# Layer 0 of a two-layer conditioned sequence block: maxima turned by a float32r product, values and weight halves copied by VectorE, several late pieces reordered

## The chip, the cores and the metric

The kernel runs on one core of a Trainium2 chip. A core has a matrix engine (TensorE, PE in the profile, with its weight loads as PEld), a vector engine (VectorE, DVE), an activation engine (ScalarE, ACT), a general engine (GpSimd, POOL), and SyncE (SP), which here only issues transfers. Each engine works off its own instructions in order, and engines wait for each other by semaphores. Operands lie in SBUF; a product goes to a PSUM bank, from which VectorE or ScalarE reads it. The metric is the device time of one execution in microseconds (us); a figure for a kernel is the median of several executions.

## The reference

The input is a batch of 32 sequences of 128 rows and 512 features, with a condition vector of 512 for each batch. Layer 0 is a normalised and modulated attention with 16 heads of 32 features, with the softmax divided once more by the root of 512; layer 1 is a single-head attention followed by a gated MLP, both modulated by the condition. All in float32.

```python
# layer 0
h   = (wg) * layernorm(x) + (wb)                # wg, wb: from the condition
q, k, v = split_heads(h @ Wqkv.T + bqkv)        # 16 heads of 32
att = softmax(q @ k.T) / sqrt(512)
h1  = (att @ v) @ Wp.T + bp + x
x   = sln(h1) + h1
# layer 1
h   = rmsnorm(x) * (1 + scale) + shift          # scale, shift: from the condition
x   = x + softmax((h @ q_w + q_b) @ (h @ k_w + k_b).T / sqrt(512)) @ (h @ v_w + v_b) @ proj_w + proj_b
h   = rmsnorm(x) * (1 + scale2) + shift2
x   = x + gelu(h @ mlp_w1 + mlp_b1) @ mlp_w2 + mlp_b2
```

## The kernel before

Products of full weight matrices run as three float32r products: each operand is split in a high half (rounded to float32r) and a low half (the rest), and high·high, low·high and high·low are added up in PSUM (`mm3`, L152). A tile of 128 partitions by 512 columns is the usual unit.

Layer 0 runs in 32 steps, `for s in range(STEPS)` (L1385 to L1486), after a prologue (L1300 to L1325). A step stands for one group of four batches (NG = 8 groups) and one chunk of four heads (KC = 4 chunks, 128 features). What one trip of the loop issues, in the text's order:

- `scores0(s)` (L633): per head row, a product of `over` (a matrix of ones in float32r) with the spread maxima `mT` into a bank `pst`, which puts the negative maximum and logarithm of the softmax under every score, and then 16 products of k and q on top.
- `energies(s + 1)`: the scores of the next step, row-wise, in four banks `pse`, and the row maxima `nm` by VectorE (L588). `totals(s + 1, r)` (L599): 16 exponentials on ScalarE that give only their row sums. `exponentials(s, ..)` (L654): ScalarE reads `pst` and gives the attention weights `e`.
- `heads_out(s - 1)` (L657): `e` times the values `v` into `pso`; ScalarE writes its high half (`o..h`, L676), VectorE the low half (`o..l`, L682).
- `logs(s + 1)` (L602 to L617): ScalarE's logarithm and exponential, some small VectorE operations, and at the end `nmx`, the maxima with their logarithms as a high and a low part, 128 rows by 4 heads by 32 columns (eight of them used, the others zero).
- `qk0(s + 2)`: the products for q and k of the step after next, read by ScalarE. Between them in steps 0 to 3 one piece of the output projection is split: `split_w` (L143), where ScalarE casts the high half `w0ph` (L145) and GpSimd takes the difference.
- `values0(s - 1 + G)` (L535): the values of one batch, in banks `psv`, which ScalarE copies to `v` (L542).
- `maxima(s + 1)` (L619 to L623): TensorE's transpose of `nmx` into `psm`; `spread_maxima` (L625): VectorE multiplies it out to `mT`.
- `End` for batch s − 4: the output projection `psp`, added to the residual `xe` by VectorE (L713). `Turned`: a coming batch is normalised (`x`, L411), cut into 16-bit halves by ScalarE, transposed by DMA on SP's queue (`tn`, L427), merged by VectorE (L432), modulated by ScalarE (L449), and split into `n..h` (L461) and `n..l` (L465) by VectorE.

Work for layer 1 and for the conditions is spread over the steps. `cond_half` (steps 3 and 4, L250 to L289) computes modulation rows with the weights `wc`, and at its end writes sums `shw` to memory and reads them back, spread over the partitions, as `shwt` (L286, L287). `l1_cq` (L790) loads `wk` in steps 7, 9, 11 and 13, and in the step after each VectorE sums it with a row (L795). In steps 29 to 31 `l1_vp` (L781) makes layer 1's value weights times its projection from chunks `w1c` into banks `psvp` (L787); `l1_load` loads further weights of layer 1.

The order is that of the text only for a part: each engine's order is set by a scheduler that lists the instructions again by their dependencies, so that an instruction may stand elsewhere in an engine's queue than its line suggests. Banks of PSUM come from small pools: `mm_tile` and `s_tile` (used for `pst`, `pso`, `psv`, `psvp`), and `e_bank` (for `pse`, `psm`, `psp`). A tile of a pool is free only when the last reader of its predecessor is done, so a late reader (`o..l` of `pso`) delays the next writer (`pst`).

Of the kernel before, what the change touches and what calls it, by code (L numbers as in the profile page):

```python
# [9 lines left out]
FP = mybir.dt.float32  # L10
# [33 lines left out]
def cond_seq_kernel(ctx: ExitStack, tc, x, condT, wcond, w0, w1, wk1, wm1, wm2, cols, rows, out):  # L44
# [42 lines left out]
    def load(t, src, by=None):  # L87
        (by or nc.sync).dma_start(out=t, in_=src)
        return t
# [13 lines left out]
    nc.gpsimd.memset(neghalf, -0.5)  # L103
    ones = const.tile([P, P], FP, name="ones")
    nc.gpsimd.memset(ones, 1.0)
    col = const.tile([P, NCOLS], FP, name="col")
# [4 lines left out]
    over = const.tile([P, P], FR, name="over")  # L111
    nc.vector.tensor_copy(over, ones)
    nmx = const.tile([P, 4, 32], FP, name="nmx")
    nc.gpsimd.memset(nmx, 0.0)

# [133 lines left out]
    def cond_half(h):  # L249
# [11 lines left out]
        def work():  # L261
            a, n = later["ca"], later["n"]
            ps = e_bank(f"psc{h}")
            for k in range(2):
                for j in range(4):
                    nc.tensor.matmul(
                        ps[32 * j : 32 * j + 32], cT[:, 2 * h + k, :], ws[j // 2][:, 2 * (j % 2) + k],
                        start=(k == 0), stop=(k == 1),
                    )
            nc.vector.tensor_tensor(a, ps, a, ALU.add)  # L270
            if h == 0:
                return
            for o in (0, 2 * B):
                nc.vector.scalar_tensor_tensor(
                    a[o : o + B], a[o : o + B], 1.0, n[o : o + B], ALU.add, ALU.mult
                )


            w, sums = l_tile("scw"), sm.tile([P, 1], FP, tag="v", name="shw")
            nc.vector.tensor_tensor(w[:B], a[:B], wu[:B], ALU.mult)  # L280
            nc.vector.scalar_tensor_tensor(
                w[B : 2 * B], a[B : 2 * B], 1.0, wu[B : 2 * B], ALU.mult, ALU.mult,
                accum_out=sums[B : 2 * B],
            )
            nc.sync.dma_start(out=scw, in_=w[:B])
            nc.sync.dma_start(out=shw, in_=sums[B : 2 * B])  # L286
            load(later["shw"], shw.rearrange("b o -> (b o)").partition_broadcast(P))  # L287

# [233 lines left out]
    def over_rows(name, acc):  # L522

        ps = e_bank(name)
        nc.tensor.matmul(ps, ones, acc, start=True, stop=True)
        return ps
# [7 lines left out]

    def values0(b, by_part=False, make=None):  # L535
        g, i = divmod(b, G)
        hT = hs[0, g][0]

        def done(ps):
            if i == 0:  # L540
                vs[g] = w_tile(f"v{g}", FP)
            nc.scalar.copy(vs[g][:, i], ps)  # L542

# [60 lines left out]
    def logs(s):  # L604
# [10 lines left out]
        t = nmx  # L615
        nc.vector.tensor_copy(t[:, :, :G].bitcast(FR), nm)
        nc.vector.tensor_tensor(t[:, :, G : 2 * G], nm, t[:, :, :G], ALU.subtract)  # L617

    def maxima(s):  # L619

        ps = e_bank(f"psm{s}")[:, :P]
        nc.tensor.transpose(ps, nmx.rearrange("p r j -> p (r j)"), ident)
        mT[s] = ps  # L623
# [32 lines left out]

    def heads_out(s):  # L657

        g, c = divmod(s, KC)
        e, v = es.pop(s), vs[g]  # L660
        if c == 0:
            os_[g] = w_pair(f"o{g}")
        pso = mm_tile(f"pso{s}")
        for i in range(G):
# [566 lines left out]
    with tc.manual_schedule(engines=ordered):  # L1231
# [80 lines left out]
        run(q)  # L1312
        totals(0, 3)
        first[0].turn()
        logs(0)
        first[0].parts()
        new.norm()
        run(k)
        new.halves()
        values = values0(2, make=mm_tile)  # L1320
        run(values[:4])
        maxima(0)
        spread_maxima(0)
        first[1].turn()
        run(values[4:])  # L1325
        first[1].parts()
# [43 lines left out]
        def vp(c):  # L1370
            l1_vp(chunk.pop(c), L1[3], c, s_tile if c < 3 else e_bank)

# [12 lines left out]
        for s in range(STEPS):  # L1385
            last = s == STEPS - 1
            end = End(s - G, True, nc.scalar) if s >= G else None
            scores0(s)
            if turned:
# [14 lines left out]
            if not last:  # L1404
                for r in range(1, 4):
                    totals(s + 1, r)
            if s:
                heads_out(s - 1)
# [27 lines left out]
            if s < KC:  # L1436
                split_w(W0["p"], raw["p"], s, nc.gpsimd)
            if s == KC + 1:
                cond_features()
            run(k)  # L1440
            if new:
                new.norm()
                new.halves()
            values = values0(s - 1 + G, make=e_bank if s < G else s_tile) if s <= B - G else []
            run(values[:9] if s < G else values)
            if s == STEPS - 3:
                vp(0)
            if s == STEPS - 2:
                vp(1)
                vp_load(3)  # L1450
                vp(2)
            if s == STEPS - 1:
# [10 lines left out]
            if past:  # L1463
                past.third()
            if "cq" in L1:
                L1.pop("cq")()
            staged = extras[s + 1]() if s + 1 in extras else None
            if end:
                run(end.stream())
                end.add()  # L1470
            if s == STEPS - 4:
                vp_load(0)
# [9 lines left out]
            if s == 2:  # L1482
                later["mods"] = r_tile("mods")
            if s == STEPS - 2:
                l1_load()
        heads_out(STEPS - 1)  # L1486
# [195 lines left out]
```

## Time and profile before

| | |
|---|---|
| median of 3 runs | 1421.9 us (1421.56 to 1423.0) |
| profiled execution, own time | 1421.69 us |
| its span in the profile | 1419.9 us, 25300 instructions |
| TensorE busy | 1402.5 us (99%), 8968 products |
| VectorE busy | 997.2 us (70%), 1970 instructions |
| ScalarE busy | 886.8 us (62%), 2386 instructions |
| GpSimd busy | 384.9 us (27%), 361 instructions |
| granted clock of TensorE | 0.999 |
| ScalarE's totals (L599) | 512 of 417 ns, and 512 reads of their sums of 257 ns |
| VectorE's row maxima (L588) | 128 of 684 ns |
| first `pst` of steps 0, 1, 2, 3, 4, 5, 6 | 50.05, 63.18, 77.22, 92.67, 107.59, 126.03, 142.77 us |
| first `pst` of steps 30 and 31 | 494.66, 510.82 us |

Busy time sums the durations of an engine's instructions. Those overlap at their ends: an instruction of 0.68 us can be followed by the next one 0.60 us after its start, so that what an instruction costs an engine is read from the distance of starts. "Idle before" is the time for which an engine stood still ahead of an instruction, with the instruction that let it go. The 1.8 us between the span and the profiled execution's own time lie before the first instruction and after the last.

### The profile page before, as it was taken

What the parts mean: (1) busy time and instruction counts of PE and PEld (TensorE: products, weight loads), DVE (VectorE), ACT (ScalarE), POOL (GpSimd) and SP (SyncE); (2) the same over time, 40 slices, a digit from 0 to 9 for tenths busy, and PEclk for the clock granted to TensorE, in tenths of its full rate; (3) what the DMA queues carried; (4) which work ended last, traced back from release to release, by engine and by line L of the source; (5) the groups of instructions that cost most, each with busy time, mean ns of one, the idle gap of its engine ahead of it and who ended that gap; (6) DMA issues with size and microseconds to landing.
All of it is one profiled execution on the core that took longest, in us unless ns stands there. A gap on an engine that the chain in (4) does not pass through costs nothing.

```text
span 1419.9 us, 25300 instructions
## 1 busy us (share of the span) xinstructions
PE 1402.5 (99%) x8968; PEld 1135.1 (80%) x8968; DVE 997.2 (70%) x1970; ACT 886.8 (62%) x2386; POOL 384.9 (27%) x361
## 2 busy tenths in 40 slices
PE   9999999999999999999999999999999999999998
PEld 5766888888888768888888888888888888888887
DVE  6666888888888887999887766665576556753342
ACT  4898899999998856677874454444453445423331
POOL 0113443535444234665541213000030003110000
PEclk9999999999999999999999999999999999999999
DMA  8359778777666557788879878576693767735350
GB/s 310 74 143 238 196 217 225 223 200 187 183 154 183 150 203 187 193 240 222 207 191 361 256 222 260 192 227 195 213 326 121 234 203 227 270 133 184 142 185 30
DMA packets 227879, 287.85 MB, mean 203 GB/s; under 512 B 107396, under 2 KB 138244, under 8 KB 226216
## 3 DMA queue, kind: packets, MB, share of 16 engines
q1 hardware_dynamic: 209888, 211.68, 51.5%
q10 hardware_dynamic: 17864, 74.55, 15.8%
q8 instruction: 70, 1.15, 0.4%
q14 instruction: 57, 0.47, 0.1%
HBM read 193.18 MB, written 73.60 MB: 188 GB/s over the span
## 4 chain that ended last, share of the span: by engine, by line
PE 87%; DMA 4%; ACT 4%; DVE 3%; issue 1%; POOL 1%; SPq 0%; ACTq 0%; POOLq 0%; DVEq 0%
PE acc L1087 24%; PE psh L165 21%; PE psp L165 6%; PE psq L165 5%; PE psk L165 5%; PE psV L165 5%; PE psv L165 5%; PE psT L165 5%; PE pso L667 2%; PE pss L848 2%; PE pse L575 2%; PE pst L644 2%; PE pso L165 1%; ACT unused L599 1%; DMA wc<-in_wcond 1%
## 5 line engine op out<-in xcount | busy, mean ns | idle before, releaser
L599 ACT ACTIVATE unused<-pse,nm 128x128 f32<-128x128 f32 x512 | 180.9, 417 | 10.3 <-DVE nm L588 7.9
L338 POOL TENSOR_TENSOR rn<-vn,neghalf 128x1 f32<-128x1 f32 x96 | 62.9, 655 | 453.3 <-DVE vn L336 346.4
L1025 ACT ACTIVATE c<-c,col 128x512 f32<-128x512 f32 x64 | 46.4, 725 | 142.3 <-DVE c L1050 89.0
L599 ACT ACTIVATION_READ_ACCUMULATOR unused<-pse,nm 128x1 f32 x512 | 131.8, 257 | 0.0
L423 ACT COPY tn<-x 128x1024 uint16<-128x1024 uint16 x90 | 94.1, 1047 | 59.2 <-DVE x L409 51.9
L432 DVE COPY tn<-tn 128x1024 uint16<-128x1024 uint16 x90 | 101.6, 1129 | 6.2 <-DMA tn<-tn 6.1
L1103 POOL TENSOR_TENSOR xe<-xe,row 128x512 f32<-128x512 f32 x32 | 45.4, 1449 | 202.8 <-DMA xe<-xs 182.9
L654 ACT ACTIVATE e<-pst 128x512 f32<-128x512 f32 x128 | 69.7, 605 | 30.1 <-PE pst L644 30.1
L588 DVE TENSOR_REDUCE nm<-pse 128x4 f32<-128x512 f32 x128 | 79.5, 684 | 11.8 <-PE pse L575 11.8
L963 POOL TENSOR_TENSOR wml<-wm,wmh 128x512 fp32r<-128x512 f32 x28 | 35.9, 1287 | 182.4 <-ACT wmh L956 154.9
L1040 DVE TENSOR_TENSOR c<-psh,ca 128x512 f32<-128x512 f32 x32 | 22.1, 692 | 86.7 <-PE psh L165 83.2
L326 DVE BATCH_NORM_STATS2 stn<-x 128x6 f32<-128x512 f32 x96 | 65.6, 683 | 2.7 <-DMA x<-in_x 2.7
L409 DVE TENSOR_SCALAR x<-x,rn 128x512 f32<-128x512 f32 x64 | 57.7, 902 | 7.4 <-POOL rn L338 6.7
L449 ACT ACTIVATE tn<-tn,mods 128x128 f32<-128x128 f32 x128 | 52.6, 483 | 11.7 <-DVE tn L432 11.7
L1053 DVE TENSOR_TENSOR ca<-psh,ca 128x512 f32<-128x512 f32 x32 | 22.1, 691 | 41.8 <-PE psh L165 41.8
L338 POOL TENSOR_TENSOR re<-ve,neghalf 128x1 f32<-128x1 f32 x32 | 31.4, 980 | 64.7 <-DVE ve L331 60.8
L1025 ACT ACTIVATE cb<-cb,col 128x512 f32<-128x512 f32 x32 | 23.2, 724 | 41.0 <-DVE cb L1054 41.0
L698 POOL TENSOR_TENSOR xe<-xe,row 128x512 f32<-128x512 f32 x32 | 44.9, 1403 | 1.7 <-DMA xe<-in_x 1.5
L1037 ACT COPY ca<-psh 128x512 f32<-128x512 f32 x32 | 18.4, 574 | 40.5 <-PE psh L165 40.0
L449 ACT ACTIVATE tn<-tn,mod 128x128 f32<-128x128 f32 x104 | 43.0, 491 | 0.0
L1107 DVE TENSOR_TENSOR xe<-acc,xe 128x512 f32<-128x512 f32 x32 | 21.1, 688 | 30.5 <-PE acc L1087 30.2
L1046 DVE TENSOR_TENSOR cb<-psh,ca 128x512 f32<-128x512 f32 x32 | 22.1, 690 | 24.8 <-PE psh L165 24.5
(1386 smaller groups left out, 4582.4 us busy)
## 6 DMA issues: line engine op xcount, KB each, us to landing
mod<-mod SPq DMA_DIRECT2D x32, 512.0 KB, 4.5
ur<-ud SPq DMA_DIRECT2D x64, 256.0 KB, 4.5
xs<-xe SPq DMA_DIRECT2D x60, 256.0 KB, 2.6
xe<-xs SPq DMA_DIRECT2D x60, 256.0 KB, 3.0
x<-xs SPq DMA_DIRECT2D x59, 256.0 KB, 3.5
scw<-scw SPq DMA_DIRECT2D x32, 256.0 KB, 3.9
hTd<-tn SPq DMA_DIRECT2D x32, 256.0 KB, 6.7
hT<-hTd SPq DMA_DIRECT2D x32, 256.0 KB, 5.1
```

Source lines behind the costliest of these rows:

```text
L165: nc.tensor.matmul(st["ps"], *calls[j], start=(j == 0), stop=(j == n - 1))
L326: nc.vector.bn_stats(st, t)
L338: nc.gpsimd.tensor_tensor(r, v, neghalf, ALU.pow)
L409: nc.vector.tensor_scalar(X, X, r, None, ALU.mult)
L423: nc.scalar.copy(halves.rearrange("p (e d) -> p e d", e=2), X.bitcast(U16).rearrange("p (d e) -> p e d", e=2),)
L432: nc.vector.tensor_copy(self.a.bitcast(U16).rearrange("p (f e) -> p e f", e=2), self.t.bitcast(U16).rearrange("p (e f) -> p e f", e=2),)
L449: nc.scalar.activation(dst[:, c], self.a[:, ts(c, P)], AF.Identity, bias=m[:, q + B : q + B + 1], scale=m[:, q : q + 1],)
L588: nc.vector.tensor_reduce(nm[:, r], chunks(banks[r]), AX.X, ALU.max, negate=True)
L599: nc.scalar.activation(unused[s][:, ts(i, P)], banks[r][:, ts(i, P)], AF.Exp, bias=nm[:, r, i : i + 1], scale=1.0, accum_out=total[:, r, i ...
L654: nc.scalar.activation(e, es[s][r], AF.Exp)
L1025: nc.scalar.activation(t[nm], t[nm], AF.Gelu, bias=col[:, C_B1 + f : C_B1 + f + 1], scale=1.0)
L1087: nc.tensor.matmul(accs[i], u[pa][:, ts(i, P)], wb[f // 4][pb][:, f % 4, :], start=(first and j == 0), stop=(last and j == len(PARTS) - 1),)
```

## The change

- `maxima`: the transpose of `nmx` against the identity becomes a product of `nmx` with `identr`, the identity cast to float32r. `nmx` is a float32r tile. The matrix `ones` is gone: `over` is cast from a tile of ones that VectorE fills, and stands for `ones` where columns are summed.
- Copies: the values of batch 2 in the prologue and those made in steps 0 to 3, and the four pieces `w0ph` of steps 0 to 3, are copied by VectorE instead of ScalarE.
- Prologue: the norm of the new batch stands ahead of the turn of the first one, the parts of the first batches are put off, and the maxima of step 0 are turned behind 8 of 12 value products instead of 4.
- Read-back: the load of `shwt` is taken out of `cond_half` and written three steps further on.
- Sums of `wk` (`cq`) behind the products and the residual addition of `End`.
- Last steps: in step 31 `heads_out(30)` stands ahead of `scores0(31)`, with a bank of `e_bank`; `vp(1)` takes a bank of `mm_tile`; `l1_load` is written between the loads and products of step 30.

```diff
@@ -101,17 +101,17 @@
     nc.scalar.preload_act_table_set("natural_log_exp_and_others")
     neghalf = const.tile([P, 1], FP, name="neghalf")
     nc.gpsimd.memset(neghalf, -0.5)
-    ones = const.tile([P, P], FP, name="ones")
-    nc.gpsimd.memset(ones, 1.0)
+    identr = const.tile([P, P], FR, name="identr")
+    nc.vector.tensor_copy(identr, ident)
     col = const.tile([P, NCOLS], FP, name="col")
     cT = const.tile([P, KC, B], FP, name="cT")
 
 
     pick = const.tile([P, G], FP, name="pick")
     over = const.tile([P, P], FR, name="over")
-    nc.vector.tensor_copy(over, ones)
-    nmx = const.tile([P, 4, 32], FP, name="nmx")
-    nc.gpsimd.memset(nmx, 0.0)
+    nc.vector.tensor_copy(over, warm[:, :P])
+    nmx = const.tile([P, 4, 32], FR, name="nmx")
+    nc.gpsimd.memset(nmx.bitcast(FP), 0.0)
 
 
     def split_sb(pair, sl, src, eng=None):
@@ -284,7 +284,6 @@
             )
             nc.sync.dma_start(out=scw, in_=w[:B])
             nc.sync.dma_start(out=shw, in_=sums[B : 2 * B])
-            load(later["shw"], shw.rearrange("b o -> (b o)").partition_broadcast(P))
 
         return work
 
@@ -522,7 +521,7 @@
     def over_rows(name, acc):
 
         ps = e_bank(name)
-        nc.tensor.matmul(ps, ones, acc, start=True, stop=True)
+        nc.tensor.matmul(ps, over.bitcast(FP), acc, start=True, stop=True)
         return ps
 
     def l0_row(got):
@@ -532,14 +531,14 @@
             row0, over_rows("psrow0", acc), ISD, bp, ALU.mult, ALU.add
         )
 
-    def values0(b, by_part=False, make=None):
+    def values0(b, by_part=False, make=None, copy=None):
         g, i = divmod(b, G)
         hT = hs[0, g][0]
 
         def done(ps):
             if i == 0:
                 vs[g] = w_tile(f"v{g}", FP)
-            nc.scalar.copy(vs[g][:, i], ps)
+            (copy or nc.scalar.copy)(vs[g][:, i], ps)
 
         return mm3(
             lambda: (make or s_tile)(f"psv{b}"),
@@ -613,13 +612,13 @@
         nc.vector.scalar_tensor_tensor(inv, total, ROOTD, inv, ALU.mult, ALU.mult)
         nc.vector.scalar_tensor_tensor(nm, inv, 1.0, nm, ALU.subtract, ALU.add, reverse0=True)
         t = nmx
-        nc.vector.tensor_copy(t[:, :, :G].bitcast(FR), nm)
-        nc.vector.tensor_tensor(t[:, :, G : 2 * G], nm, t[:, :, :G], ALU.subtract)
+        nc.vector.tensor_copy(t[:, :, :G], nm)
+        nc.vector.tensor_tensor(t[:, :, G : 2 * G], nm, t[:, :, :G].bitcast(FP), ALU.subtract)
 
     def maxima(s):
 
         ps = e_bank(f"psm{s}")[:, :P]
-        nc.tensor.transpose(ps, nmx.rearrange("p r j -> p (r j)"), ident)
+        nc.tensor.matmul(ps, nmx.rearrange("p r j -> p (r j)"), identr, start=True, stop=True)
         mT[s] = ps
 
     def spread_maxima(s):
@@ -654,13 +653,13 @@
             nc.scalar.activation(e, es[s][r], AF.Exp)
             es[s][r] = e
 
-    def heads_out(s):
+    def heads_out(s, make=mm_tile):
 
         g, c = divmod(s, KC)
         e, v = es.pop(s), vs[g]
         if c == 0:
             os_[g] = w_pair(f"o{g}")
-        pso = mm_tile(f"pso{s}")
+        pso = make(f"pso{s}")
         for i in range(G):
             for r in range(4):
                 rr = slice(32 * r, 32 * r + 32)
@@ -1311,18 +1310,18 @@
         q, k = qk0(1)
         run(q)
         totals(0, 3)
+        new.norm()
         first[0].turn()
         logs(0)
-        first[0].parts()
-        new.norm()
         run(k)
+        first[1].turn()
         new.halves()
-        values = values0(2, make=mm_tile)
-        run(values[:4])
+        values = values0(2, make=mm_tile, copy=nc.vector.tensor_copy)
+        run(values[:8])
         maxima(0)
         spread_maxima(0)
-        first[1].turn()
-        run(values[4:])
+        run(values[8:])
+        first[0].parts()
         first[1].parts()
         W0["p"] = w_pair("w0p")
 
@@ -1368,7 +1367,7 @@
             chunk[c] = l1_chunk(2, c)
 
         def vp(c):
-            l1_vp(chunk.pop(c), L1[3], c, s_tile if c < 3 else e_bank)
+            l1_vp(chunk.pop(c), L1[3], c, (s_tile, mm_tile, s_tile, e_bank)[c])
 
         FIRST1 = STEPS - G - 2
 
@@ -1385,6 +1384,8 @@
         for s in range(STEPS):
             last = s == STEPS - 1
             end = End(s - G, True, nc.scalar) if s >= G else None
+            if last:
+                heads_out(s - 1, e_bank)
             scores0(s)
             if turned:
                 turned.high(nc.vector.tensor_copy)
@@ -1404,7 +1405,7 @@
             if not last:
                 for r in range(1, 4):
                     totals(s + 1, r)
-            if s:
+            if s and not last:
                 heads_out(s - 1)
             if s == STEPS - 2:
                 vp_load(2)
@@ -1434,20 +1435,27 @@
             if staged:
                 staged()
             if s < KC:
-                split_w(W0["p"], raw["p"], s, nc.gpsimd)
+                split_w(W0["p"], raw["p"], s, nc.gpsimd, nc.vector.tensor_copy)
             if s == KC + 1:
                 cond_features()
+            if s == KC + 3:
+                load(later["shw"], shw.rearrange("b o -> (b o)").partition_broadcast(P))
             run(k)
             if new:
                 new.norm()
                 new.halves()
-            values = values0(s - 1 + G, make=e_bank if s < G else s_tile) if s <= B - G else []
+            values = []
+            if s < G:
+                values = values0(s - 1 + G, make=e_bank, copy=nc.vector.tensor_copy)
+            elif s <= B - G:
+                values = values0(s - 1 + G)
             run(values[:9] if s < G else values)
             if s == STEPS - 3:
                 vp(0)
             if s == STEPS - 2:
                 vp(1)
                 vp_load(3)
+                l1_load()
                 vp(2)
             if s == STEPS - 1:
                 vp(3)
@@ -1462,12 +1470,12 @@
                 ready.rest()
             if past:
                 past.third()
-            if "cq" in L1:
-                L1.pop("cq")()
             staged = extras[s + 1]() if s + 1 in extras else None
             if end:
                 run(end.stream())
                 end.add()
+            if "cq" in L1:
+                L1.pop("cq")()
             if s == STEPS - 4:
                 vp_load(0)
             coming_new = None if last else coming(s + 1)
@@ -1481,8 +1489,6 @@
                 L1["cq"] = l1_cq(CQ.index(s))
             if s == 2:
                 later["mods"] = r_tile("mods")
-            if s == STEPS - 2:
-                l1_load()
         heads_out(STEPS - 1)
         heads_high(STEPS - 1)
         heads_low(STEPS - 1)
```

## The prediction

> **What bounds the kernel now.** I read the chain of waits first, then busy time by stretch, then the timelines of the engines where the change lands. A difference of 0.2% (2.8 us of 1421.9) is about what a measurement of this kernel can tell from no change; "same" below means within it.
>
> The chain of waits by engine, and two stretches (columns: stretch, its length, then busy us and instructions of TensorE (PE), its weight loads, VectorE (DVE), ScalarE (ACT), GpSimd; granted clock; DMA share; GB/s):
>
> ```profile
> PE 87%; DMA 4%; ACT 4%; DVE 3%; issue 1%; POOL 1%; SPq 0%; ACTq 0%; POOLq 0%; DVEq 0%
> ...
> 55.00:100.00 45.00, 40.97 (x425) 31.02 (x428) 31.18 (x68) 41.47 (x154) 6.74 (x7) 1.00 0.47 98
> ...
> 260.00:340.00 80.00, 80.00 (x864) 65.16 (x864) 68.41 (x145) 73.52 (x267) 36.27 (x33) 1.00 0.73 198
> ```
>
> TensorE ends most of the span, and from step 6 of layer 0 on it has no hole (80.00 of 80.00): steps there last 14.53 to 14.57 us from one pst to the next. So a cost on TensorE counts in full in some 28 steps, work on other engines counts in steps 0 to 5 (TensorE 40.97 of 45.00), at step 9 and in the last two. After step 31 TensorE runs on without a gap, so what a step gains or loses stays to the end.
>
> In the early steps ACT has the larger share (41.47), but a share doesn't tell who waits. VectorE's timeline across the end of step 1 does (start, duration, line, and in brackets idle time before):
>
> ```profile
> 75.72 0.17 DVE L617 TENSOR_TENSOR nmx<-nm,nmx 128x16 f32<-128x16 f32 x1
> 75.81 0.54 DVE L411 TENSOR_SCALAR x<-x,mvn,rn 128x512 f32<-128x512 f32 x1
> 76.38 0.69 DVE L628 TENSOR_TENSOR mT<-psm,pick 128x512 fp32r<-128x512 f32 x1
> 76.99 0.68 DVE L682 TENSOR_TENSOR o0l<-pso,o0h 128x512 fp32r<-128x512 f32 x1
> 77.59 1.17 DVE L520 TENSOR_SCALAR wrow<-w0rp,col 128x512 f32<-128x512 f32 x1
> ...
> 82.09 2.48 DVE L588 TENSOR_REDUCE nm<-pse 128x4 f32<-128x512 f32 x4
> ...
> 92.44 0.68 DVE L682 TENSOR_TENSOR o0l<-pso,o0h 128x512 fp32r<-128x512 f32 x1
> 95.17 0.43 DVE L461 CAST n_8h<-tn 128x512 fp32r<-128x512 f32 x1 [2.05 <-ACT tn L449]
> ```
>
> From 75.72 to 84.5 VectorE never stops, and the row maxima (nm) that close this run are what ACT's totals wait for (82.87, 1.24 idle before them, released by DVE). Only at 95.17 does VectorE wait, for ACT.
>
> **The product in place of the transpose.** Each step turns the maxima once (psm, 32 times). Its neighbours in a steady step, then the nearest product by shape:
>
> ```profile
> 271.34 0.39 PE L165 MATMUL psv<-w0vh,n_16l 128*128 128x512 f32 x1
> 271.57 0.33 PE L622 MATMUL psm<-ident,nmx 128*128 128x128 f32 x1
> 271.66 0.48 PE L165 MATMUL psp<-w0ph,o2h 128*128 128x512 f32 x1
> 271.97 0.40 PE L165 MATMUL psp<-w0pl,o2h 128*128 128x512 f32 x1
> ...
> L848 PE MATMUL pss<-n_0f,T x32: 270/275/275, 554.2 to 557.7; 128*128 128x128 f32 x32
> ```
>
> The psv products are float32r and follow each other by 0.228 us for 512 columns. From psv at 271.34 to the second psp at 271.97 are 0.63, of which two wide products are 0.455: the transpose, with the slower start behind it, is worth 0.175 here, and 0.116 in steps whose psm loads its weights early (the same sum with psp 0.026 behind psm). No float32r product of 128 columns is in the trace. If time goes by columns, it takes a quarter of 0.228, 0.057, in place of 0.108 (the spacing of the other transposes, pstn): −0.05 a step. At the other end stands the fp32 product of the same 128x128 shape (pss), whose 32 take 3.6 us with two records each, 0.224 a piece: +0.116, or +0.16 if its weight load (0.19 in pss against 0.138 in psm) shows as well. Over 28 steps: −1.4 to +4.5. I take the row of the same shape, pss, with a little of the weight load: +0.125 a step, **+3.5**. This is the least certain term.
>
> [...] No run shows yet what a float32r product does here.
>
> **Prologue.** The turn of maxima 0 now stands behind 8 value products instead of 4, and the values of batch 2 are copied by VectorE:
>
> ```profile
> 47.51 0.33 PE L622 MATMUL psm<-ident,nmx 128*128 128x128 f32 x1 [0.81 <-DVE nmx L617]
> ...
> 50.83 0.78 PE L640 MATMUL pst<-mT,over 32*128 32x512 f32 x3 [0.29 <-ACT v L542]
> ```
>
> The 0.81 goes, because four more products (0.91) cover it. The copy on VectorE, idle there, ends near 49.85, ahead of the new pst. Step 0 starts its totals 0.93 earlier: **−0.93**.
>
> **Copies moved from ACT to VectorE, steps 0 to 3.** Each step moves a weight copy w0ph (ACT 0.61, start to start 0.51) and a value copy v (ACT 0.59, 0.47). On VectorE the first is a cast from SBUF like n_4h (0.42, start to start 0.43), the second reads PSUM like mT and o0l (0.68, 0.60). In the built order w0ph stands behind nmx, v between mT and o_l or the weighted sums: VectorE does 1.03 more per step ahead of the next nm.
> Step 0: VectorE is continuously busy from 61 to 69.6, so the 0.93 of the prologue is eaten: nm comes at its old time (+0.0 to +0.1).
> Step 1: 0.43 + 0.60 with 0.1 of slack ahead of an unbroken run: nm, totals and logs +0.93.
> Step 2: inherits 0.93. o0l, which frees the bank of the next pst, now lies behind w0ph and v, so pst goes from 93.27 to 95.2 (+1.95). n_8h had waited 2.05 there for ACT, and ACT has become faster, which absorbs most of the rest: nm +1.13, not +1.95.
> Step 3: v waits for the last psv, o0l queues behind v, and pst behind o0l: +2.5. Here there is no cover.
> SP's queue: a transpose by DMA (for batch 10) now stands between the halves of a conditioning weight that landed at 115.63 after 7.5 us and for which psc1 stalled 1.3. Issued 110.9 to 112.5 it lands at 116 to 120 against the stream's own +2.5; stall 0 to 2.4. In step 5 the next transposed batch (landing 137.68, then the merge, nmx and a psm stalled 1.53) shifts with the stream. I carry **+2.5** out of step 5, with 1.6 and 4.0 as ends.
>
> **The put-off read-back.** The load of shwt moves by three steps in the text, but in the built order it keeps its place on SP, straight ahead of the transpose at 128.07: **0**. If it did leave SP's queue there, that transpose could go earlier and the stall of 1.53 with it.
>
> **The layer-1 column sums (wk) behind the residual add.** At step 9:
>
> ```profile
> 187.14 0.69 DVE L795 SCALAR_TENSOR_TENSOR wk<-wk,row 128x512 f32<-128x512 f32 x1
> ...
> 187.75 0.69 DVE L713 TENSOR_TENSOR xe<-psp,xe 128x512 f32<-128x512 f32 x1
> ```
>
> xe comes 0.61 earlier, its psum bank is free sooner, and the stall of 0.48 of the energies behind it goes; that step lasts 15.45 against 14.55. **−0.6** (0 to −0.9; nothing reads wk soon).
>
> **Last steps.**
>
> ```profile
> 500.15 3.70 PE L787 MATMUL psvp<-w1r,w1c 128*128 128x512 f32 x8 [1.60 <-ACT e L654]
> 504.34 3.67 PE L787 MATMUL psvp<-w1r,w1c 128*128 128x512 f32 x8 [0.49 <-DMA w1c<-in_w]
> ...
> 513.06 1.08 PE L667 MATMUL pso<-e,v 128*32 128x128 f32 x32 [0.49 <-ACT e L654]
> ```
>
> The first psvp gets another bank and may start at 498.5, but the second still waits for a chunk landing at 504.20, issued at 495.30 behind two loads of 1 MB, and in the built order the l1_load that the text moves up stays where it was: 0 to −0.3, I take 0. The last pso now precedes the last pst, so its 0.49 and most of the ordering loss go: psvp at 514.07 becomes 513.05, **−1.05** (0 to −1.1).
>
> The other edits (one cast of the identity, a memset less, the ones matrix taken from over) lie in the first microseconds, under the loads: 0; uncovered, 0.4.
>
> **Sum.** The profiled run took 1421.69 for a span of 1419.9, 0.2 below the median 1421.9, which I neglect. The moved copies' +2.5 holds the prologue's −0.93 already. 1421.69 + 2.5 + 0 − 0.6 − 1.05 = 1422.5 without the product; with it, **1425.9**.
>
> **The rivals.**
> 1. The product is cheap, by columns: 1422.5 − 1.4 = 1421.1, or 1422.5 if it costs what the transpose did: same. For it: the wide float32r products run at 0.228 where fp32 takes two records of 0.43. Against: nothing as narrow is shown.
> 2. Faster: ACT ends the early steps, not VectorE. Each of four steps then returns 0.98 of ACT's time (0.47 + 0.51): −3.9, with −0.6 and −1.05: 1416.1 with a free product, 1419.6 with the dear one. For it: ACT busy 41.47 of 45.00, and VectorE waits 2.05 for ACT at 95.17. Against: the unbroken run to 84.5, with ACT idle 1.24 behind it. It decides where VectorE's added 1.03 falls into its idle time rather than ahead of nm and o0l, in at least three of the four steps.
> 3. The conditioning weight arrives late and adds up to 1.5 to the forecast: 1427.4.
>
> **How the numbers follow.** Forecast 0.45, its own range 1424.2 to 1427; rival 3 0.08; rival 1 0.25; rival 2 0.22. Faster by over 0.2% is below 1419.1: most of rival 2 (0.15) and rival 1 with the copies at their low end (0.04), 0.19. Same, up to 1424.7: the rest of rival 1 (0.21) and some of rival 2 with a dear product (0.07), 0.28. Slower: the forecast and rival 3, 0.53. The range, 1418.2 to 1428.2, leaves out most of rival 2's cheap half and the worst of the weight's delay.
>
> **What would show it.** Steady steps of 14.65 instead of 14.55 between psts (product dear) or 14.50 (cheap). VectorE's order nmx, w0ph, x, mT, v, o0l, and pst of steps 3 and 4 some 2 us late; if these psts come early, rival 2. Step 9 near 14.6. The wait at the psvp pair moved from e to the chunk. pso ahead of pst at the end. Wrong altogether I would be if TensorE's steady spacing were not what carries those 400 us.

## The result, and the profile after

The changed kernel takes 1425.8 us (median of 14 runs, 1423.6 to 1429.55), the kernel before 1423.22 us in the same session (1420.94 to 1424.69): ratio 1.0021, 95% interval [1.0013, 1.0029]. It is slower, by 2.6 us between the medians. The profiled run has a span of 1423.9 us against 1419.9.

Where the 4.0 us between the two spans lie, read from the first `pst` of each step and the first product of layer 1 (`psT`):

| stretch | before | after | difference |
|---|---|---|---|
| up to step 0 | 50.05 | 50.17 | +0.12 |
| steps 0 to 2 | 42.62 | 43.38 | +0.76 |
| step 3 | 14.92 | 16.88 | +1.96 |
| step 4 | 18.44 | 22.60 | +4.16 |
| step 5 | 16.74 | 15.13 | −1.61 |
| steps 6 to 29 | 351.89 | 351.81 | −0.08 |
| step 30 to layer 1 | 26.78 | 25.68 | −1.10 |
| the rest | | | −0.2 |

The time was lost in steps 3 and 4. The 24 steps from 6 on, which the forecast charged with a dear product, cost nothing on balance: step 9 gives back 0.75, and the others together lose 0.68. The chain of waits and the two stretches of the changed kernel (columns as before: length, busy us and instructions by engine, granted clock, DMA share, GB/s):

```profile
PE 94%; DVE 2%; ACT 2%; DMA 1%; issue 0%; ACTq 0%; SPq 0%; DVEq 0%
...
55.00:100.00 45.00, 39.53 (x411) 30.38 (x410) 30.79 (x69) 36.20 (x135) 7.17 (x6) 0.96 0.39 97
260.00:340.00 80.00, 80.00 (x835) 64.86 (x834) 67.60 (x146) 73.19 (x256) 32.95 (x30) 1.00 0.75 205
```

ScalarE is indeed relieved (36.20 of 45 for 41.47), and TensorE does less in the same stretch, not more. The new figure stands ahead of the DMA share: a granted clock of 0.96. Cut finer, first the changed kernel and then the one before:

```profile
90.00:95.00 5.00, 2.75 (x15) 1.54 (x17) 4.06 (x11) 4.32 (x11) 1.50 (x1) 1.00 0.23 57
95.00:98.00 3.00, 3.00 (x61) 3.00 (x60) 1.12 (x2) 1.52 (x4) 0.00 (x0) 0.51 0.49 95
118.00:122.00 4.00, 1.93 (x16) 0.40 (x16) 1.53 (x1) 3.97 (x23) 1.32 (x2) 1.00 1.06 337
122.00:125.00 3.00, 3.00 (x10) 1.39 (x6) 2.31 (x8) 1.28 (x4) 0.00 (x0) 0.56 0.06 16
```

```profile
90.00:95.00 5.00, 4.10 (x66) 2.89 (x69) 2.96 (x8) 5.00 (x11) 1.38 (x1) 1.00 0.84 142
95.00:98.00 3.00, 2.88 (x56) 2.27 (x52) 2.79 (x5) 2.09 (x9) 0.00 (x0) 1.00 0.53 53
```

Twice TensorE has holes (2.75 busy of 5, 1.93 of 4), and each time the clock that it is granted falls to one half right behind them. Summed over single microseconds, the clock missing is 1.71 us from 95 to 99 and 1.70 us from 122 to 126: 3.41 us at one half each time. Before, no such stretch lies inside the kernel; only the last 1.7 us of the span, behind TensorE's last product, run at half.

The holes themselves, on TensorE (start, duration, idle time before; `psc` is the bank of `cond_half`'s products):

```profile
91.56 0.30 PE L621 MATMUL psm<-identr,nmx 128*128 128x128 f32 x1 [0.59 <-DVE nmx L616]
...
93.55 0.47 PE L639 MATMUL pst<-mT,over 32*128 32x512 f32 x1 [0.94 <-DVE mT L627]
94.74 0.54 PE L639 MATMUL pst<-mT,over 32*128 32x512 f32 x3 [0.73 <-DVE o0l L681]
...
121.08 2.38 PE L266 MATMUL psc<-wc,cT 128*32 128x512 f32 x10 [2.08 <-DMA wc<-in_wcond]
123.39 0.80 PE L165 MATMUL psk<-n_4h,w0kh 128*128 128x512 f32 x1
123.99 0.63 PE L165 MATMUL psk<-n_4l,w0kh 128*128 128x512 f32 x1
```

In the kernel before, the same places:

```profile
92.67 1.10 PE L640 MATMUL pst<-mT,over 32*128 32x512 f32 x4 [0.65 <-DVE mT L628]
...
115.67 1.90 PE L266 MATMUL psc<-wc,cT 128*32 128x512 f32 x10 [0.24 <-DMA wc<-in_wcond]
```

The first pair waits for VectorE, in the order that the forecast read from the built program (here at the end of step 1; steps 2 and 3 have the same, with one more operation between `nmx` and `w0ph`):

```profile
76.15 0.18 DVE L616 TENSOR_TENSOR nmx<-nm,nmx 128x16 fp32r<-128x16 f32 x1
76.24 0.42 DVE L145 CAST w0ph<-w0rp 128x512 fp32r<-128x512 f32 x1
76.58 0.54 DVE L410 TENSOR_SCALAR x<-x,mvn,rn 128x512 f32<-128x512 f32 x1
77.03 0.68 DVE L627 TENSOR_TENSOR mT<-psm,pick 128x512 fp32r<-128x512 f32 x1
77.63 0.68 DVE L541 COPY v<-psv 128x512 f32<-128x512 f32 x1
78.23 0.68 DVE L681 TENSOR_TENSOR o0l<-pso,o0h 128x512 fp32r<-128x512 f32 x1
```

`w0ph` stands ahead of mT and v ahead of `o0l`, and `pst` waits for both. The last hole waits for the second half of the last piece of `wc`, which is called wc11 below, and SP's queue shows why it came late:

```profile
110.36 0.33 SPq L88 DMA_DIRECT2D wc<-in_wcond  x1
111.21 2.44 SPq L426 DMA_TRANSPOSE tn<-tn  x1
113.71 0.59 SPq L88 DMA_DIRECT2D wc<-in_wcond  x1
```

Before, both halves were issued by 108.5, ahead of the transpose:

```profile
107.37 1.12 SPq L88 DMA_DIRECT2D wc<-in_wcond  x2
108.61 2.85 SPq L427 DMA_TRANSPOSE tn<-tn  x1
```

Now the first is issued at 110.36, because its buffer is that of the raw projection weight, which GpSimd reads last, and GpSimd starts behind the copy that VectorE makes:

```profile
108.81 1.53 POOL L146 TENSOR_TENSOR w0pl<-w0rp,w0ph 128x512 fp32r<-128x512 f32 x1 [5.95 <-DVE w0ph L145]
```

In the kernel before:

```profile
105.83 1.51 POOL L146 TENSOR_TENSOR w0pl<-w0rp,w0ph 128x512 fp32r<-128x512 f32 x1 [5.07 <-ACT w0ph L145]
```

The second half is issued 5.6 us later than before and lands at 121.04, for 115.63 before. Not all of this is the copy's doing, as the whole stream is later here: step 4 begins at 110.43 instead of 107.59. The run u_w0ph3 below tells the two apart.

The end of layer 0 and step 9 went as forecast. The residual addition is ahead of the column sum, and the last pso ahead of the last pst:

```profile
192.00 0.69 DVE L712 TENSOR_TENSOR xe<-psp,xe 128x512 f32<-128x512 f32 x1 [0.25 <-issue]
192.61 0.68 DVE L794 SCALAR_TENSOR_TENSOR wk<-wk,row 128x512 f32<-128x512 f32 x1
```

```profile
509.50 3.67 PE L786 MATMUL psvp<-w1r,w1c 128*128 128x512 f32 x8 [2.00 <-ACT unused L598]
...
515.94 1.08 PE L666 MATMUL pso<-e,v 128*32 128x128 f32 x32
516.95 0.51 PE L639 MATMUL pst<-mT,over 32*128 32x512 f32 x4
```

The bracket at 509.50 names ScalarE, but the chunk `w1c` landed at 509.36: the two waits of 1.60 and 0.49 have become one of 2.00.

### The profile page after: what moved, and what is told of

Its sections match the earlier page's. It is cut to its first block, busy times and chain, and to the rows that moved or that the text cites. A ratio compares the mean times of both kernels' runs of the same rounds, so it can differ in the third digit from the quotient of the medians.

```text
span 1423.9 us, 25301 instructions
## 1 busy us (share of the span) xinstructions
PE 1406.1 (99%) x8968; PEld 1138.5 (80%) x8968; DVE 1000.3 (70%) x1980; ACT 883.4 (62%) x2377; POOL 384.4 (27%) x360
## 4 chain that ended last, share of the span: by engine, by line
PE 94%; DVE 2%; ACT 2%; DMA 1%; issue 0%; ACTq 0%; SPq 0%; DVEq 0%
PE acc L1086 24%; PE psh L165 21%; PE psV L165 6%; PE psT L165 6%; PE psp L165 6%; PE psq L165 6%; PE psk L165 5%; PE psv L165 5%; PE pss L847 2%; PE pso L666 2%; PE pst L643 2%; PE pse L574 2%; PE pso L165 2%; ACT unused L598 2%; PE psm L763 1%; PE pst L639 1%
## 5 line engine op out<-in xcount | busy, mean ns | idle before, releaser
L1102 POOL TENSOR_TENSOR xe<-xe,row 128x512 f32<-128x512 f32 x32 | 45.3, 1447 | 202.1 <-DVE u_7s L1078 117.1
L697 POOL TENSOR_TENSOR xe<-xe,row 128x512 f32<-128x512 f32 x32 | 45.0, 1408 | 0.6 <-DMA xe<-in_x 0.6
L899 POOL TENSOR_TENSOR xe<-xe,row 128x512 f32<-128x512 f32 x28 | 39.1, 1404 | 1.3 <-ACT V L126 1.3
```

## The experiments

Each ratio is to the kernel before, measured beside it; step lengths are from the profile of that kernel.

### The transpose in place of the product (u_turn)

```diff
-        nc.tensor.matmul(ps, nmx.rearrange("p r j -> p (r j)"), identr, start=True, stop=True)
+        nc.tensor.transpose(ps, nmx.rearrange("p r j -> p (r j)"), ident)
```

> The changed kernel with the maxima turned by the transpose again, all else kept. Theory (a float32r product of 128 columns costs TensorE what the transpose did, 0.122 against 0.117 where the weights come early, and its longer weight load, 0.186 against 0.138, shows as 0.04 to 0.05 in the other steps): some 27 steps give back about 1.1 us, ratio to before about 1.0013. Rival (the forecast's term: a product of this kind takes 0.125 more a step): 3.5 us come back, ratio 0.9997 or below, and steady steps go from 14.57 to 14.45.

1424.06 us, ratio 1.0013 [1.0004, 1.0022]. Steps 16 to 24 last 14.543 on the mean, against 14.557 in the changed kernel and 14.541 before; other kernels here that keep the product have 14.564 to 14.573. So the product costs 0.016 to 0.03 a step, not 0.125, some 0.4 to 0.8 us in all. The ratio fits the theory; its interval overlaps that of the changed kernel, and it is the steps' lengths that decide: the five profiles with the transpose lie between 14.539 and 14.543, the eight with one product between 14.557 and 14.573.

This run also prices the clock. Its wc11 is as late as in the changed kernel (stall 2.23), but the clock stays full behind the stall, and step 4 lasts 21.13 instead of 22.60.

### The product twice (p_twice)

```diff
         nc.tensor.matmul(ps, nmx.rearrange("p r j -> p (r j)"), identr, start=True, stop=True)
+        nc.tensor.matmul(ps, nmx.rearrange("p r j -> p (r j)"), identr, start=True, stop=True)
```

> The changed kernel with the product of the maxima issued twice in each step, the second over the first. Each steady step then shows what one more float32r product of 128 columns costs TensorE. Theory (time by columns with the weight load half hidden): 0.06 to 0.12 a step. Rival (the forecast: four times as slow for so few columns): 0.22 to 0.30 a step.

One execution alone, 1427.97 us, without a ratio. Steps 16 to 24 last 14.681: one product more costs 0.11 to 0.12. TensorE's rows of one step:

```profile
276.33 0.33 PE L621 MATMUL psm<-identr,nmx 128*128 128x128 f32 x1
276.50 0.27 PE L622 MATMUL psm<-identr,nmx 128*128 128x128 f32 x1
276.61 0.45 PE L165 MATMUL psp<-w0ph,o2h 128*128 128x512 f32 x1
```

The second product starts 0.17 after the first and psp 0.11 behind it. That is what a transpose costs, half of what the forecast took. It lies between the two ends, at twice a quarter of a wide product. Whether the columns or its own weight load (0.186) make it so, this run doesn't tell.

### The copies back on ScalarE, each alone (u_w0ph, u_w0ph3, u_v)

```diff
-                split_w(W0["p"], raw["p"], s, nc.gpsimd, nc.vector.tensor_copy)
+                split_w(W0["p"], raw["p"], s, nc.gpsimd)
```

> The changed kernel with the four weight copies w0ph on ScalarE again. SP's queue then holds both halves of wc11 ahead of the transpose of batch 10, as before. Theory (the w0ph copy of step 3, behind nmx and ca on VectorE, releases the buffer of wc11 3 us late and lets the transpose in between, so that the second half lands at 121.04 and psc stalls 2.08): the stall falls below 0.6, step 4 lasts at most 19.5 instead of 22.60, step 5 gives back some of it (back to about 16.5), and the whole is 1.5 to 3 us faster than the changed kernel: ratio to before 1.000 to 1.001. Rival (the w0ph copies cost only by VectorE's time in steps 1 to 3): step 4 keeps its stall of 2 us and steps 1 to 3 lose 0.4 each.

1422.92 us, ratio 1.0008 [0.9999, 1.0017]. Step 4 falls from 22.60 to 18.59 and psc runs through, since SP now has both halves ahead of the transpose. But step 5 takes 19.60, where 16.5 was expected: the transposed batch 11 then lands late for its merge, psm waits 1.90, and the clock falls to half from 141 to 145. The theory of step 4 holds; what step 5 gives back was underrated.

With the copy of step 3 alone back on ScalarE:

```diff
-                split_w(W0["p"], raw["p"], s, nc.gpsimd, nc.vector.tensor_copy)
+                split_w(W0["p"], raw["p"], s, nc.gpsimd, nc.vector.tensor_copy if s < KC - 1 else None)
```

> The changed kernel with only the last of the four weight copies, that of step 3, on ScalarE again. Same queue order on SP as with all four. Theory (it is the copy of step 3 alone, by the queue and the late release): step 4 at most 19.5, whole as with all four back within 0.5 us. Rival (VectorE's time in each of the steps): a quarter of what all four bring, and the stall of psc stays.

1424.14 us, ratio 1.0014 [1.0005, 1.0023]. Step 4 lasts 18.70: this one copy, by the order on SP, makes the stall of psc. The release of the buffer has little part in it: counted from the first `pst` (49.09 here, 50.17 in the changed kernel), the first half is issued 0.4 us sooner than there, the second, at 109.24, 3.4 us sooner. So most of the 3 us by which GpSimd starts later than in the kernel before is the lateness of the stream. Step 5 gives back most of the gain (18.11, with waits of 1.35 at pso and 1.44 at psm). Steps 1 to 3 stay at 14.53, 15.70 and 16.79, with the clock at half from 93 to 97. That the whole comes within 0.5 us of the one with all four back was not met in the medians (1.2), though their intervals overlap.

```diff
-                values = values0(s - 1 + G, make=e_bank, copy=nc.vector.tensor_copy)
+                values = values0(s - 1 + G, make=e_bank)
```

> The changed kernel with the value copies of steps 0 to 3 on ScalarE again (that of the prologue stays on VectorE). Theory (v stands ahead of o_l on VectorE and pst waits for o_l): the waits of pst for o_l in steps 2 to 4 (0.73, 0.73, 0.88) fall to about 0.15, step 2 to 4 starts come some 0.6 earlier each at most 1.5 in all, but the stall of psc for wc11 stays and takes most of it back: ratio to before 1.001 to 1.002. Rival (ScalarE's time decides): step 2 to 4 get longer by 0.4 each, ratio 1.003.

1423.18 us, ratio 1.0007 [0.9998, 1.0016]. Steps 2 and 3 fall to 15.10 and 14.75, and there is no half clock in step 3: taking v off VectorE shortens the holes (pst waits 0.13 for `o0l` instead of 0.73). Whether other runs keep the clock there too isn't shown: the mean clock over the 11 runs is 0.9976, hardly above the changed kernel's 0.9972. The gain was larger than expected (step 5 begins 3.5 us sooner, 1.3 of it from the start), and the ratio lies just below the range given. Step 4 lasts 23.25, as its late weight has a longer stall of 3.39, and the clock is at half from 119 to 122 behind it.

### The read-back put off in fact (s_before, s_after, s_w)

In the built order the changed line did not move the load. Here it is held by a dependency:

```diff
             if s == KC + 3:
+                nc.gpsimd.tensor_copy(later["shw"][:, :1], end.X[:, :1])
                 load(later["shw"], shw.rearrange("b o -> (b o)").partition_broadcast(P))
```

> The kernel before with the read-back of shwt held back for good: GpSimd first copies one column of step 7's residual tile into shwt, so that the load can't be issued sooner (that column is then overwritten by the load). Nothing else changes. Theory (the read-back, which waits for the sums to land in memory, holds up the transposed batch 11 behind it on SP, and that batch's merge stands on VectorE ahead of the logarithms): the transpose is issued 3 to 4 us sooner, the stall of 1.53 at psm of step 5 goes, step 5 lasts about 15.2 instead of 16.74, ratio 0.9989. Rival (the transfer of batch 11 is slow anyway, since other loads share the engines): step 5 keeps 16.5, ratio 1.000.

1427.49 us, ratio 1.0018 [1.0007, 1.0030]: slower, and the theory fell. The transpose is issued 2.3 us sooner, as wanted, and its merge waits longer than ever (SP, ScalarE's queue, VectorE, TensorE of this run):

```profile
125.73 3.52 SPq L426 DMA_TRANSPOSE tn<-tn  x1
...
125.94 0.61 ACTq L1478 DMA_DIRECT2D w2d<-in_wm  x1
...
142.54 1.82 DVE L431 COPY tn<-tn 128x1024 uint16<-128x1024 uint16 x1 [5.35 <-DMA tn<-tn]
...
145.27 0.45 PE L621 MATMUL psm<-ident,nmx 128*128 128x128 f32 x1 [4.88 <-DVE nmx L616]
```

Issued 0.2 us from a 1 MB copy in memory (`w2d`), the transpose takes 16.8 us to land, against 9.6 in the kernel before, where it follows the copy by 4. Step 5 lasts 21.56. Five of the twelve runs lie between 1421.6 and 1425.1 and seven between 1427.4 and 1429.1, and the profile is of the second group, so this shows what can happen and not what always does. Step 4, too, lasts longer here (20.01): psc waits 1.82, because the second half of wc11 lands 9.0 us after its issue instead of 7.5, with SP's queue up to there in the order of the kernel before. So a late landing can come without a change of order.

> The changed kernel with the read-back of shwt held back in the same way. Theory (in the changed kernel the late weight wc11 has taken the place of that stall: step 5 lasts 15.13 there already): the 2 us stall of psc in step 4 stays, step 5 gains at most 0.5, ratio 1.0017 to 1.0021. Rival (the put-off read-back was worth its 1.5 us in either kernel): ratio about 1.001.

1426.05 us, ratio 1.0017 [1.0008, 1.0026], as the theory had it: step 4 at 22.83, step 5 at 15.13. Here the transpose is issued 1.5 us ahead of w2d and lands in 8.2.

> The changed kernel with the read-back held back and the four w0ph copies on ScalarE. Theory (two stalls that cover one another: the late wc11 and the late batch 11; with both gone TensorE runs through): step 4 at most 18.8 and step 5 at most 15.8 (19.60 with the copies alone), some 3.5 us off the kernel with the copies alone, ratio 0.998 to 0.9990. Rival (step 5's loss there has another cause, as o_l or e): step 5 stays over 18, ratio 1.000 to 1.001.

The read-back held and `w0ph` on ScalarE: 1424.65 us, ratio 1.0022 [1.0007, 1.0036], missed. Step 4 lasts 19.90 and step 5 16.81, and the runs scatter from 1422.53, which is the profiled one, to 1432.03. The transpose again runs beside w2d (13.7 us to landing), psc waits 0.96 with both halves ahead of the transpose of batch 10, and the clock is at half from 78 to 81.

### The transfers put right (c_wc, c_before, c_dve, c_best)

One transfer for each pair of halves of wc:

```diff
-        for j in range(4):
-            load(ws[j // 2][:, 2 * (j % 2) : 2 * (j % 2) + 2], wcond[:, 2 + j, 2 * h : 2 * h + 2])
+        for j in range(2):
+            load(ws[j].rearrange("p (j k) d -> p j k d", j=2), wcond[:, 2 + 2 * j : 4 + 2 * j, 2 * h : 2 * h + 2])
```

> The changed kernel with each pair of halves of the conditioning weights loaded by one transfer of 1 MB, so that the transpose of batch 10 can't come between the halves of wc11; the copies stay on VectorE. Theory (of the 5.6 us by which the second half is issued later, 3 come from the late release of its buffer and 2.6 from the transpose in between): the load is issued near 110.4 and lands near 118 to 119, the stall of psc in step 4 falls from 2.08 to under 1, step 4 to 21 at most, step 5 goes up from 15.13 to some 16, and the whole gains 0.5 to 1.5: ratio 1.001 to 1.0017. Rival (the stall comes from the DMA engines' load, not from the order): landing still at 121, step 4 over 22, ratio 1.002.

1424.21 us, ratio 1.0020 [1.0010, 1.0030]. The stall of psc is gone (step 4 18.61, more than expected), so it was the transfer in between. The whole gained nothing: step 5 takes 18.19 with waits of 1.34 at pso and 1.56 at psm, and the clock stays at half from 92.8 to 99.6.

Read-back held, and w2d a step later, in the kernel before:

```diff
-            q2, late = divmod(s - W_FIRST, 3)
+            q2, late = divmod(s - W_FIRST - 1, 3)
```

> The kernel before with the read-back held back and the 1 MB copies w2d, issued by ScalarE in steps 4, 7, 10 and 13, one step later each. Theory (with the read-back held back alone, the transpose of batch 11 was issued 0.2 us from w2d and shared the DMA engines with it, 16.8 us to landing; without w2d beside it, it lands some 8 us after its issue): step 5 falls from 21.56 to about 15.2, psm waits for nothing, whole 3 to 6 us faster than with the read-back alone and 1.5 faster than the kernel before, ratio 0.9985 to 0.9993. Rival (the transpose is late by the mod and x loads ahead of it): step 5 stays over 18, ratio 1.001 or more.

1419.8 us, ratio 0.9987 [0.9979, 0.9996]: step 5 lasts 15.15, and psm waits for nothing. The neighbour of the transpose made the difference, not its place behind the read-back alone. It landed after 11.0 us, not the 8 expected, which was soon enough.

> The changed kernel with all three transfers put right (read-back held back, w2d a step later, wc in one load) and the copies still on VectorE. Theory (the copies on VectorE cost about 2.7 us in steps 1 to 3 by themselves, 1.5 more in step 4's pst and the late weight): steps 1 to 3 as in the changed kernel (14.5, 15.7, 16.9), step 4 at 20 to 21, step 5 15.2, ratio 0.9995 to 1.001. Rival (all of the loss is the transfers'): steps 1 to 3 shrink too, ratio 0.998 or less.

The changed kernel with all three transfers mended: 1423.21 us, ratio 1.0007 [0.9998, 1.0016]. Steps 4 and 5 are down to 18.38 and 15.60, steps 1 to 3 keep 14.53, 15.69 and 16.85, with the clock at half from 93 to 97. So the copies on VectorE cost 2.7 us in these steps by themselves (60.24 for steps 0 to 3, against 57.54 before), holes and clock together.

> The changed kernel with the transpose for the maxima, both copies on ScalarE again in steps 0 to 3, the read-back held back, w2d a step later and wc in one load; the prologue, the column sums behind the addition and the last steps stay as changed. Theory: prologue 1.1 sooner, steps 1 to 3 as before (14.0, 15.4, 14.9), step 4 at 18.0 to 18.5, step 5 at 15.2, step 9 at 14.7, the last steps 1.1 shorter: 4 to 5 us below the kernel before, ratio 0.9965 to 0.9975. Rival (other transfers take the place of w2d in step 5): step 5 or 6 over 16, ratio 0.998 to 0.9995.

The mended transfers, the transpose for the maxima, both copies on ScalarE, and the rest of the change: 1417.89 us (1416.92 to 1419.7), ratio 0.9972 [0.9962, 0.9983], the fastest here and faster than both kernels. Its profile at the places shown above:

```profile
90.00:94.00 4.00, 3.22 (x71) 2.46 (x69) 1.94 (x5) 4.00 (x9) 1.37 (x1) 1.00 0.77 106
94.00:97.00 3.00, 2.87 (x45) 2.24 (x41) 2.97 (x6) 2.09 (x11) 0.00 (x0) 1.00 0.21 45
118.00:126.00 8.00, 8.00 (x88) 6.57 (x90) 6.51 (x14) 4.50 (x9) 0.00 (x0) 1.00 0.65 49
126.00:140.00 14.00, 13.68 (x109) 10.72 (x109) 10.56 (x25) 13.44 (x49) 7.12 (x6) 1.00 0.99 235
```

The clock is full throughout. Steps 0 to 3 take 57.35, steps 4 and 5 33.45 (35.18 before).

## Why the prediction came out as it did

The forecast of 1425.9 met the median, and the sign was right, but the number is luck, twice over. Two of its terms were wrong and cancelled: step 6 begins 5.4 us late where +2.5 had been forecast, and from there to step 30 the kernel gains 0.08 where the product less the column sums should have cost about 2.9. And the forecast was a rise of 4.2 over the 1421.69 of one profiled run; beside the changed kernel the kernel before came to 1423.22, so the measured rise is 2.6. (The terms as written add up to 1426.0.)

- **The product**: forecast +3.5 (0.125 a step), found 0.016 to 0.03 a step, 0.4 to 0.8 in all. The step that failed is the choice of the row of the same shape, 0.224: a float32r product so narrow costs 0.11 to 0.12 (p_twice), like the transpose that it replaced (0.108 to 0.116). The rival that had it so (1422.5) was right on this point.
- **The copies on VectorE**: the mechanism was right. The order, the place in front of `o0l`, the waits of pst for it (0.73 in steps 2 and 3 and 0.88 in step 4, each 0.13 before) came as written. ScalarE's relief did end waits (pso had waited 0.81 and 0.87 for e in steps 1 and 2, now 0.22 and nothing), but the new ones were longer. From the first pst on, 3.4 us had been forecast to the end of step 5 (2.5 and the prologue's 0.93), and 5.3 came. What the sum lacked is the clock: 1.71 us of it missing in step 3 and 1.70 in step 4, which stand on no row of the kernel before, where TensorE is busy for 4.10 of the 5 us from 90 on (2.75 here). In time this is somewhat less. Of the 1.96 that step 3 lost, 0.77 are longer waits, which leaves 1.2; a second stretch of the same length in c_wc made that step 1.16 longer. Step 4 with the late weight but a full clock is 1.5 shorter (u_turn, p_twice). Taking the clock (2.7), the late weight (1.84) and the stall that went in step 5 (−1.53) from the 5.3, an estimate of 2.3 is left for the waits alone, less than the 3.4 forecast. A step paid 0.94 for the copies (0.34 and 0.60 from start to start), for 1.03 forecast.
- **The weight wc11** came late, as the third rival had it: stall 2.08, 1.84 more than before, inside the 0 to 2.4 given. (Before, psc stood still for 0.24; the prediction's 1.3 is the distance of two starts, 114.37 to 115.67.) Its second half was issued at 113.71 and landed at 121.04, both later than the 110.9 to 112.5 and 116 to 120 given. Step 4 is accounted for by this, the clock's 1.5 to 1.7 and the longer wait for `o0l` (0.75): 4.1 to 4.3 for a measured 4.16. In step 5 the old stall of 1.53 at psm disappeared, because the stream had become later (7.0 us at the start of step 5) than the transposed batch (issued 4.0 us later); the forecast had kept it.
- **The prologue**: 0.93 forecast. In nine of eleven profiles with this prologue pst starts at 48.8 to 49.1, against 50.05 to 50.63 in the three with the old one, 0.9 to 1.8 sooner. In the profile of the changed kernel (50.17) and of s_after (50.24) the gain doesn't show, because their first weight products ran late (first eight 6.04 us in the changed kernel, 3.87 before). An estimate is that the clock made them late: in the changed kernel these products start 0.85 us apart up to 9.40 and 0.43 apart from 10.00 on, and the trace's record of the clock begins, at full, at 9.73; in the kernel before they start 0.43 apart from 5.38 on, and the record begins at 5.05. In s_after each microsecond from 6 to 9 holds parts of three products, in u_turn each one from 6 to 8 parts of four.
- **The read-back**: 0 forecast and 0 found, as it kept its place. The remark that moving it would free the stall of 1.53 was wrong as it stood: alone it made the kernel slower, and only with w2d out of the way did it gain.
- **The column sums**: −0.6 forecast, −0.75 found in step 9. Against this, steps 11, 13 and 15 became 0.12 to 0.15 longer, with the transpose as with the product (14.67 to 14.69 in the best kernel). Of the gain −0.35 is left, and the forecast had no term for the rest.
- **The last steps**: −1.05 forecast, −1.10 found, and the wait moved from e to the chunk as written.

What stays open: where the clock falls in a run that was not profiled. In the profile of the changed kernel 3.4 us of clock are missing in the two stretches and 0.5 behind TensorE's last product, a mean of 0.997. The mean over its 14 runs is 0.9972, and 0.9997 over the 33 runs of the kernel before that stood beside the first group, a difference of 3.6 us of clock in 1424. So a usual run lacks about as much as the profiled one, but what that costs depends on where it falls. Why steps 11, 13 and 15 became longer is open too.

## What to carry to other kernels

Moving work from a busy engine to a less busy one must be priced at its place in the queue: here 0.94 us a step went in front of the two operations for which TensorE waits. Look, too, at what the moved operation releases: one copy on the other engine frees the buffer of a load, and in the built order a transfer then stood between the halves of that load, which cost more than the copy's own time (step 4 lasted 22.60 us with it and 18.70 without it, for a copy of 0.42). And short waits of TensorE that lie close together had a price of their own: behind waits of 0.59, 0.94 and 0.73 us the granted clock stood at 0.50 for 3.41 us, an estimated 1.2 us of time, so a sum of waits alone was too low.

## What the runs showed of the hardware

- Holes of 0.59, 0.94 and 0.73 us within 4 us (2.75 busy of 5), or one of 2.08, were followed by 3.41 us at a granted clock of 0.50, with 1.7 us of clock missing each time. In one kernel (c_wc) it lasted 6.83, from 92.8 to 99.6, although TensorE was busy for 2.39 of the 3 us from 93 on. Similar holes of 2 us in step 30 were followed by it in three kernels (s_after, c_wc, c_dve: 3.4 us at 0.50 from 511.4, 509.2 and 506.6) and not in others (2.00 in the changed kernel), and the 2.23 of u_turn in step 4 were not either, so it doesn't follow from the length of a hole alone. Where a trace has more than one such stretch, their starts lie whole multiples of 3.413 us apart (27.3 in the changed kernel, 416.4 in c_wc, 413.0 in c_dve). What decides which hole is followed by one isn't shown.
- A transpose by DMA of 256 KB took 8.2 to 16.8 us from issue to landing: 8.2 when issued 1.5 us ahead of the 1 MB copy (s_after), 9.6 when 4 us behind it (before), 10.1 to 10.6 when 2.6 to 3.7 us behind it (u_turn, p_twice, c_wc), 11.0 to 11.2 without it (c_before, c_dve, c_best), 13.7 and 16.8 when issued within 0.3 us of it (s_w, s_before). Other loads ran beside it in each, so this is no rule for the distance alone.
